# A group's feed-forward moved into the last beats of a delta rule, with the quantized layer two groups behind

## The chip, the core and the metric

The kernel runs as one program on one core of a Trainium2 chip. The metric is the device time of one execution in microseconds. Engine names are those of the profile: PE (TensorE matmul), PEld (its weight loads), DVE (VectorE), ACT (ScalarE), POOL (GpSimd), SP (SyncE, which here only issues DMAs).

## The reference

The input x is 16 sequences of 128 tokens with 256 features, all in float32. The computation is

```
a  = causal attention of x (16 heads of 16, a temperature per sequence)
x1 = x + delta_rule(a)          # gated delta rule: 16 key heads, 32 value heads of 128,
                                # causal convolution of 4 taps, chunks of 64, gated norm, W_out
f  = lora_ffn(x1, adapter of the sequence)
       gate = x1 Wg + (x1 Ag[i]) Bg[i];  up = x1 Wu + (x1 Au[i]) Bu[i]     # 256 -> 1024, rank 16
       h    = silu(gate) * up
       f    = h Wd + (h Ad[i]) Bd[i]                                       # 1024 -> 256
q  = quantized_ffn(f)           # weights rounded to float8 e4m3, 256 -> 768 -> 256
out = x1 + q
```

i is one of 8 adapters, drawn for each sequence.

## The kernel before

**Groups and units.** The 16 sequences are worked on in four groups (`NG`) of four (`GS`), 512 tokens each (`GT`). The delta rule has 64 units: 16 key heads for each group, in the order of groups. Everything is float32, so that TensorE takes two instructions for each product of a 128x128 block with 512 columns.

**The written order.** A beat of the delta rule (`BEAT`, 24 units of plan time) starts one unit. The steps of a unit have due times in `TIMES`, counted from its start: keys 0 to 32.5, decays, the inverse of a lower triangle for four units at once, mergers 178 to 187, `last` 194, values 177 to 195.5, outputs 217 to 236, finish 244 to 255.5. `plan` puts steps in a heap by due time and `run` issues them in that order, so in one beat steps of up to eleven units lie beside each other. The tile framework allocates the buffers, sets all semaphores, and fixes each engine's order when the program is compiled: by program order as a priority, and by when it reckons inputs and buffers to be ready. VectorE's order is tied to program order by hand (class `InOrder`, V). On ScalarE `silu_of` and `logarithms` tie the Silus and the blocks of Ln and Exp into an order, since they need different function tables.

**The end of a unit.** `attend` makes the outputs of a unit and their squares, `root` sums the squares, `share` (SP queue) writes the roots to DRAM (`scales`) and reads them back to all partitions as `rb`, 512 KB. `norm` (line 864, POOL) multiplies z by rb, and `project` (line 873, PE, 16 instructions) adds the unit's share of W_out to PSUM. After a group's last unit x is added and x1 is stored to DRAM (line 879).

**The buffers.** Pools are stacked. The delta rule's pools are c2 (cw, nw), w2 (w_qk), pc (Uc and Tc, cv, aT in 9 buffers, bT in 7, and small ones) and the `late` pools behind it (W, T, w_v, w_gate, wo_head, v, z, y, rb, x_in and others). ps_b has six PSUM buffers, ps_r two. `pa` and `keep` lie below them and stay. A pool opened after these are closed lies on the same addresses and waits for the last users of what it covers.

**The stage after.** `ffn_loads` is issued when the last inverse is done (plan time 1632). It loads wg and wu, the adapters of group 0 and x1 of group 0 into pa's buffers. After the delta rule's pools are closed, w3 (weights), p3 (work) and eight PSUM buffers (ps_x, ps_g) are opened. `adapted(g)` is the feed-forward with adapters in 14 steps: `turn` twice (transposes of x1, line 1074, and a copy to x1T), `low` (line 1081, and a mask on DVE), eight times `hidden` (lines 1091 and 1095; Silu on ACT, product on DVE), `low_down` (line 1106, and a mask), `down` twice (lines 1115 and 1116). `quantized(g)` has six `fuse` steps (lines 1134 and 1139) and two `down` (line 1148). `rounding` is nine steps that round the quantized weights with `qm` as scratch, on DVE and POOL; `behind` puts them after a product of `hidden`. `next_adapter(g)` gathers the adapters of a group by five indirect DMAs on POOL (lines 905 and 907) and rearranges them by a copy on ACT (line 910). `merge` interleaves lists evenly:

```python
for g in range(NG + 1):
    lists = []
    if g < NG:
        lists.append(adapted(g))
    if g == 0:
        lists.append([lambda: None] * 3 + [lambda f=f: behind(f) for f in rounding])
    else:
        lists.append(quantized(g - 1))
    if g + 1 < NG:
        lists.append(next_adapter(g + 1))
    merge(*lists)
```

So group 0 runs beside the rounding, groups 1 to 3 each beside the quantized part of the group before, and the quantized part of group 3 by itself.

Of the kernel before, what the change touches and what calls it, by code (L numbers as in the profile page):

```python
# [17 lines left out]
P = 128  # L18
# [40 lines left out]
def tile_adaln_attn_ffn(  # L59
# [108 lines left out]
    def attention():  # L168
# [47 lines left out]
        def project(g):  # L216
# [15 lines left out]

            def queries(e):
                if e == 0:
                    d["q"] = pc.tile([P, ND, GT], F32, name="qT", tag="Uc", bufs=2)
                A.copy(d["q"][:, e, :], product(wq_sb, e))

            def vals(i):
                if i == 0:
                    d["v"] = pc.tile([P, GS, D], F32, name="vt", tag="Tc", bufs=2)  # L240
# [366 lines left out]
    def inverse(n):  # L607
# [293 lines left out]

    def adapter(g, t, raw):

# [8 lines left out]
    def residual(g, t):  # L912
        nc.sync.dma_start(out=t, in_=x1[g * GS : (g + 1) * GS].rearrange("b s d -> s b d"))
        pre["x", g] = t

    pre = {}

# [49 lines left out]
    for n in range(N + LAST + 1):  # L967
# [37 lines left out]
        run(BEAT * (n + 1))  # L1005
        if n == N + 1 + int(TIMES["inverse"][-1] // BEAT):
            ffn_loads()
    run(BEAT * (N + LAST + 9))
    late["stack"].close()
    st.close()  # L1010


    with ExitStack() as st:
        w3 = st.enter_context(tc.tile_pool(name="w3", bufs=1))
        p3 = st.enter_context(tc.tile_pool(name="p3", bufs=2))
        ps_x = st.enter_context(tc.tile_pool(name="ps_x", bufs=4, space=PSUM))
# [16 lines left out]


        def quantize(t, n):
            m = w3.tile([P, QI * ND], F32, name="qm", tag="qm")[:, :n]

            def step():
                V.tensor_scalar(m.bitcast(I32), t.bitcast(I32), 0x7F800000, None, ALU.bitwise_and)
# [6 lines left out]
            def checked():  # L1046
# [11 lines left out]
        grp3 = {}  # L1058

        def masked(dst, ps):  # L1060

            V.tensor_tensor(dst.rearrange("p (s t) -> p s t", t=S), ps.rearrange("p (s t) -> p s t", t=S),
                            fourth[:, :, None].to_broadcast([P, GS, S]), ALU.mult)

        def adapted(g):
            d = grp3[g] = {}

            def turn(c):
                if c == 0:
                    d["x"] = p3.tile([P, ND, GT], F32, name="x1T", tag="x1T")  # L1070
                    d["h"] = p3.tile([P, NFI, GT], F32, name="hid", tag="hid", bufs=1)
                ps = ps_x.tile([P, GS, S], F32, name="ps_xt", tag="x")
                for s in range(GS):
                    T.transpose(ps[:, s, :], pre["x", g][:, s, c * P : (c + 1) * P], ident)  # L1074
                A.copy(d["x"][:, c, :], ps.rearrange("p s t -> p (s t)"))

            def low():
                ps = ps_x.tile([P, GT], F32, name="ps_low", tag="x")
                for c in range(ND):
                    w = pre["a", g][:, 2 * c : 2 * c + 2].rearrange("p j s r -> p (j s r)")  # L1080
                    T.matmul(ps, lhsT=w, rhs=d["x"][:, c, :], start=c == 0, stop=c == ND - 1)  # L1081
                d["low"] = p3.tile([P, GT], F32, name="low", tag="low")
                masked(d["low"], ps)

            def hidden(i):
                cols = slice(i * P, (i + 1) * P)
                both = []
                for w in ("wg", "wu"):
                    ps = ps_g.tile([P, GT], F32, name="ps_gu", tag="g")
                    for c in range(ND):  # L1090
                        T.matmul(ps, lhsT=pre[f"{w}{c}"][:, cols], rhs=d["x"][:, c, :], start=c == 0, stop=False)  # L1091
                    both.append(ps)

                for ps, half in zip(both, HALVES):
                    T.matmul(ps, lhsT=pre["b", g][half, cols], rhs=d["low"][half, :], start=False, stop=True)  # L1095
                gs = p3.tile([P, GT], F32, name="gs", tag="gs")
                A.activation(gs, both[0], AF.Silu)
                grp3["product"] = V.tensor_tensor(d["h"][:, i, :], both[1], gs, ALU.mult)

            def low_down():  # L1100


                ps = ps_x.tile([P, GT], F32, name="ps_ld", tag="x")
                for i in range(NFI):
                    w = pre["a", g][:, 2 * ND + i].rearrange("p s r -> p (s r)")
                    T.matmul(ps[HALVES[i % 2]], lhsT=w, rhs=d["h"][:, i, :], start=i < 2, stop=i >= NFI - 2)  # L1106
                d["ld"] = p3.tile([P, GT], F32, name="ld", tag="ld")
                masked(d["ld"], ps)
                d["y"] = p3.tile([P, ND, GT], F32, name="yT", tag="yT")

            def down(e):
                ps = ps_x.tile([P, GT], F32, name="ps_y3", tag="x")
                cols = slice(e * P, (e + 1) * P)
                for i in range(NFI):
                    T.matmul(ps, lhsT=wd_sb[:, i, cols], rhs=d["h"][:, i, :], start=i == 0, stop=False)  # L1115
                T.matmul(ps, lhsT=pre["b", g][:, FI + e * P : FI + (e + 1) * P], rhs=d["ld"], start=False, stop=True)  # L1116
                A.copy(d["y"][:, e, :], ps)

            return (
                [lambda: turn(0), lambda: turn(1), low]  # L1120
                + [lambda i=i: hidden(i) for i in range(NFI)]
                + [low_down, lambda: down(0), lambda: down(1)]
            )

        def quantized(g):
            d = grp3[g]
# [32 lines left out]
            with tc.issue_after(grp3["product"].ins):  # L1159
                f()  # L1160

        def next_adapter(g):
            d = grp3["next"] = {}

            def gather():
                d["arrange"] = adapter(g, p3.tile([P, GS * LA + LB], F32, name="adapters", tag="adapters"),
                                       w3.tile([P, GS * LA], F32, name="firsts", tag="firsts"))

            return [gather, lambda: d["arrange"]()]
# [76 lines left out]
```

## Time and profile before

| what | value |
|---|---|
| time, median of 3 runs | 2249.76 us (2246.99 to 2257.99) |
| the profiled execution: time, span | 2258.01 us, 2256.3 us |
| mean granted clock of TensorE | 0.98 |
| PE busy | 2127.2 us, 94% of the span, 15992 instructions |
| PEld busy | 1297.5 us, 58% |
| DVE busy | 1404.9 us, 62% |
| ACT busy | 1365.7 us, 61% |
| POOL busy | 831.6 us, 37% |
| DMA | 182.14 MB, 81 GB/s in the mean |

The profile is of one execution; its times start at the first instruction. PE's busy time is modelled from the instructions' starts, so overlapping matmuls count as one stretch. A line such as L873 is a line of the kernel; L79 is the helper that issues every operation of VectorE, so there the tile's name tells what it is. `x16` is a number of instructions. In brackets stand the idle time of the engine before an instruction and what ended it.

### The profile page before, as it was taken

To read this page: it belongs to the slowest core of one execution; us is meant where nothing else is said; L and a number is where in the kernel's file an instruction comes from. 1 tells how busy PE (TensorE), PEld (TensorE's weight loads), DVE (VectorE), ACT (ScalarE), POOL (GpSimd) and SP (SyncE) were. 2 spreads that over 40 slices of the span, in tenths; PEclk is the share of its full clock that TensorE was granted. 3 is DMA by queue.
4 is the path that set the end of the run, shared out by engine and by line. 5 is a ranking of instruction groups with operands and counts; after the bars stand their busy time and mean duration, and the time that the engine had idled before them with its cause. 6 is when DMAs were issued, how large, how long until landed. Compare 5 with 4: busy or idle time off the path is not lost. (4 is left out here: it accounts for less than half of the span.)

```text
span 2256.3 us, 41245 instructions
## 1 busy us (share of the span) xinstructions
PE 2127.2 (94%) x15992; PEld 1297.5 (58%) x15992; DVE 1404.9 (62%) x2194; ACT 1365.7 (61%) x2373; POOL 831.6 (37%) x573
## 2 busy tenths in 40 slices
PE   7898689999999999999999999999998987999999
PEld 3444356666666666666666666666665663344445
DVE  4788887677686867768686777868665321311111
ACT  4778577777777777777777777777775661111110
POOL 2233535445262544526254452625444115400000
PEclk9999889999999999999999999999999998999999
DMA  2210123333334434333433433334333314000000
GB/s 60 70 44 25 55 64 88 96 103 100 96 107 113 112 93 107 98 97 107 114 111 93 107 99 96 106 101 115 93 103 94 99 56 153 0 5 17 10 5 14
DMA packets 303250, 182.14 MB, mean 81 GB/s; under 512 B 189393, under 2 KB 283345, under 8 KB 303057
## 3 DMA queue, kind: packets, MB, share of 16 engines
q1 hardware_dynamic: 300848, 175.00, 28.0%
q0 software_dynamic: 1344, 4.20, 0.6%
q8 instruction: 128, 2.10, 0.4%
q14 instruction: 66, 0.53, 0.1%
q10 hardware_dynamic: 864, 0.31, 0.1%
HBM read 152.69 MB, written 5.77 MB: 70 GB/s over the span
## 5 line engine op out<-in xcount | busy, mean ns | idle before, releaser
L79 DVE SCALAR_TENSOR_TENSOR cv<-ps_in,cw,cv 128x508 f32<-128x508 f32 (+2 forms) x768 | 567.1, 740 | 297.4 <-ACT cv L476 279.3
L873 PE MATMUL ps_out<-wo_head,z 128*128 128x256 f32 x1024 | 251.7, 390 | 35.7 <-POOL z L864 35.5
L864 POOL TENSOR_TENSOR z<-z,rb 128x1024 f32<-128x1024 f32 x64 | 151.2, 2362 | 310.9 <-DMA rb<-scales 264.7
L467 PE MATMUL ps_in<-hT,w_qk 128*128 128x512 f32 x512 | 249.0, 610 | 5.3 <-DVE cv L79 2.4
L467 PE MATMUL ps_in<-hT,w_v 128*128 128x512 f32 x512 | 248.6, 607 | 0.0
L873 PEld LDWEIGHTS ps_out<-wo_head,z 128*128 128x128 f32 x1024 | 190.7, 194 | 99.6 <-POOL z L864 67.8
L812 PE MATMUL ps_z<-hT,w_gate 128*128 128x512 f32 x512 | 241.9, 594 | 0.3 <-ACT M L776 0.3
L476 ACT ACTIVATE cv<-ps_in,cw 128x512 f32<-128x512 f32 x256 | 174.9, 683 | 77.9 <-PE ps_in L467 76.3
L638 POOL TENSOR_TENSOR prod<-lanes,inv 128x512 f32<-128x512 f32 (+1 forms) x64 | 129.5, 2045 | 121.3 <-DVE inv L79 121.3
L525 POOL TENSOR_TENSOR o<-off,lk 128x16 f32<-128x16 f32 x64 | 13.9, 217 | 414.8 <-ACT lk L555 414.8
L812 PEld LDWEIGHTS ps_z<-hT,w_gate 128*128 128x128 f32 x512 | 95.8, 190 | 114.4 <-issue 101.1
L829 PEld LDWEIGHTS ps_ot<-aT,y 128*128 128x128 f32 x1024 | 134.5, 192 | 38.1 <-issue 28.5
L586 PE MATMUL ps_kq<-kq 128*128 128x256 f32 x512 | 134.8, 407 | 15.4 <-DVE cv L79 14.0
L467 PEld LDWEIGHTS ps_in<-hT,w_qk 128*128 128x128 f32 x512 | 94.1, 195 | 85.9 <-issue 66.5
L823 PEld LDWEIGHTS ps_y<-v,W 128*128 128x128 f32 x1024 | 124.5, 192 | 30.6 <-issue 22.9
L570 ACT ACTIVATE kq<-cv 128x512 f32<-128x512 f32 x128 | 80.7, 630 | 97.8 <-DVE cv L79 97.6
L829 PE MATMUL ps_ot<-aT,y 128*128 128x128 f32 x1024 | 135.6, 275 | 1.7 <-ACT y L824 1.7
L638 POOL TENSOR_TENSOR prod<-inv,gm 128x512 f32<-128x512 f32 (+1 forms) x64 | 127.9, 2023 | 15.3 <-DVE gm L79 15.3
L823 PE MATMUL ps_y<-v,W 128*128 128x128 f32 x1024 | 124.8, 275 | 0.0
L467 PEld LDWEIGHTS ps_in<-hT,w_v 128*128 128x128 f32 x512 | 87.5, 190 | 64.1 <-issue 61.2
L529 POOL TENSOR_TENSOR aT<-aT,o 128x1024 f32<-128x1024 f32 x64 | 121.8, 1902 | 5.1
L586 PEld LDWEIGHTS ps_kq<-kq 128*128 128x128 f32 x512 | 94.7, 197 | 34.5 <-issue 9.4
(202 smaller groups left out, 4069.0 us busy)
## 6 DMA issues: line engine op xcount, KB each, us to landing
aT<-sums SPq DMA_DIRECT2D x64, 512.0 KB
rb<-scales SPq DMA_DIRECT2D x64, 512.0 KB
w_qk<-in_w_qkv_dram SPq DMA_DIRECT2D x128, 128.0 KB
w_v<-in_w_qkv_dram SPq DMA_DIRECT2D x64, 256.0 KB
w_gate<-in_w_z_dram SPq DMA_DIRECT2D x64, 256.0 KB
wo_head<-in_w_out_dram SPq DMA_DIRECT2D x64, 256.0 KB
diag<-bT SPq DMA_DIRECT2D x256, 32.0 KB
W<-Uc SPq DMA_DIRECT2D x256, 32.0 KB
```

The source lines that it names most:

```text
L79: ins = getattr(self.engine, name)(*args, **kw)
L467: T.matmul(ps, lhsT=w[:, c, blk, :], rhs=hTs[g][:, c, :], start=c == 0, stop=c == ND - 1)
L476: A.activation(cv, psv, AF.Copy, scale=cw[:, col, 3:4])
L529: G.tensor_tensor(t4, t4, o.rearrange("p s h i -> p (s h) i")[:, :, :, None].to_broadcast([P, NP, 2, C]), ALU.subtract)
L570: ins = A.activation(dst, src, AF.Silu)
L586: T.matmul(ps[:, j, :, :], lhsT=d["kq"][:, s, 0, :], rhs=d["kq"][:, s, :, :], start=True, stop=True)
L638: G.tensor_tensor(out_tile, lhs[:, :, None, :].to_broadcast([P, r, c, j]), rhs.rearrange("p j c -> p c j")[:, None, :, :].to_broadcast([P, ...
L812: T.matmul(ps, lhsT=w_gate[u][:, c, h * P : (h + 1) * P], rhs=hTs[g][:, c, :], start=c == 0, stop=c == ND - 1)
L823: T.matmul(ps[:, j, :], lhsT=d["W"][:, p, :], rhs=v[:, p, :], start=True, stop=True)
L829: T.matmul(ps[:, s * S : (s + 1) * S], lhsT=d["y"][:, 2 * s + h, :], rhs=d["aT"][:, 2 * s + h, :], start=True, stop=True)
L864: G.tensor_tensor(d["z"], d["z"], d["rb"], ALU.mult)
L873: T.matmul(ps[:, j, :], lhsT=d["z"][:, h, s * S : (s + 1) * S], rhs=w_o[u][:, h, :], start=kh == j == h == 0, stop=kh == NK - 1 and j == h ...
```

## The change

1. Group 0's feed-forward with adapters (`adapted(0)`) is no longer in the stage after. Its 14 steps are planned into the delta rule's last beats at due times of their own (`DRAIN_TIMES`, 1639.2 to 1758.6). It works in the delta rule's buffers (class `Drain`): PSUM from ps_b; x1T, the two low ranks, the gates and the down weights in bT's buffers, the hidden rows in aT's, and its result yT in one of hT's.
2. The down weights wd are loaded for it in two halves of 512 KB (plan times 1689.6 and 1692), and once more as wd_sb after the delta rule as before.
3. x1 of group 1 is loaded in `ffn_loads`, into the buffer of `off`.
4. Uc and Tc get a pool of their own, pi, ahead of pc. After the delta rule the order of pools is w0 (adapters, 2 buffers, and their raw form), p2 (x1T, hid, low, gs, ld of groups 1 to 3), w3, p3. `next_adapter(1)` is issued first there.
5. `qm` has three buffers instead of one.
6. The stage after runs over g = 1 to 5: group 1 beside the rounding, group 2 beside the quantized part of group 0, group 3 beside that of group 1, then the quantized parts of groups 2 and 3 one after the other.

`adapted`, `masked` and `next_adapter` are otherwise as they were: buffers come from an object `room`, which is a `Drain` or a `Rest`.

```diff
@@ pools
     w2 = st.enter_context(tc.tile_pool(name="w2", bufs=2))
+    pi = st.enter_context(tc.tile_pool(name="pi", bufs=2))
     pc = st.enter_context(tc.tile_pool(name="pc", bufs=1))
...
-                    bt["T"] = pc.tile([P, BL, BL], F32, name="Tc", tag="Tc", bufs=2)
+                    bt["T"] = pi.tile([P, BL, BL], F32, name="Tc", tag="Tc")
...
-            bt["U"] = pc.tile([P, BL, BL], F32, name="Uc", tag="Uc", bufs=2)
+            bt["U"] = pi.tile([P, BL, BL], F32, name="Uc", tag="Uc")
...
@@ ffn_loads
         residual(0, pa.tile([P, GS, D], F32, name="x1_in", tag="diag"))
+        residual(1, keep.tile([P, GS, D], F32, name="x1_in", tag="off", bufs=1))
...
+    def adapted(g, room):
+        d = grp3[g] = {}
+        def turn(c):
+            if c == 0:
+                d["x"] = room.x()
+                d["h"] = room.hidden()
+            ps = room.ps("ps_xt", "x").rearrange("p (s t) -> p s t", t=S)
...
+        def hidden(i):
...
+                ps = room.ps("ps_gu", "g")
...
+            gs = room.gs(i)
+            A.activation(gs, both[0], AF.Silu)
+            grp3["product"] = V.tensor_tensor(d["h"][i], both[1], gs, ALU.mult)
...
+        def down(e):
+            ps = room.ps("ps_y3", "x")
+            cols = slice(e * P, (e + 1) * P)
+            for i in range(NFI):
+                T.matmul(ps, lhsT=room.down(i)[:, cols], rhs=d["h"][i], start=i == 0, stop=False)
...
+    class Drain:
+        def __init__(self):
+            self.both = {}
+        def ps(self, name, tag):
+            return ps_b.tile([P, GT], F32, name=name, tag="b")
+        def x(self):
+            return pc.tile([P, ND, GT], F32, name="x1T", tag="bT", bufs=7)
+        def hidden(self):
+            parts = [pc.tile([P, 2, GT], F32, name="hid", tag="aT", bufs=9) for _ in range(NFI // 2)]
+            return [parts[i // 2][:, i % 2, :] for i in range(NFI)]
+        def half(self, name, i):
+            if name not in self.both:
+                self.both[name] = pc.tile([P, 2, GT], F32, name=name, tag="bT", bufs=7)
+            return self.both[name][:, i, :]
+        def low(self, name):
+            return self.half("lows", 0 if name == "low" else 1)
+        def gs(self, i):
+            return self.half("gs", i % 2)
+        def y(self):
+            return keep.tile([P, ND, GT], F32, name="yT", tag="hT", bufs=2)
+        def load_down(self, i):
+            t = self.both["wd", i] = pc.tile([P, 4, D], F32, name="wd_sb", tag="bT", bufs=7)
+            nc.sync.dma_start(out=t, in_=wd.rearrange("(c p) e -> p c e", p=P)[:, 4 * i : 4 * i + 4])
+        def down(self, i):
+            return self.both["wd", i // 4][:, i % 4, :]
...
+    DRAIN_TIMES = [1639.2, 1644.0, 1648.2, 1653.0, 1662.6, 1672.2, 1681.8, 1699.8, 1699.8, 1717.8, 1729.8, 1739.4, 1749.0, 1758.6]
...
         if n == N + 1 + int(TIMES["inverse"][-1] // BEAT):
             ffn_loads()
+            drain = Drain()
+            plan(0, adapted(0, drain), DRAIN_TIMES)
+            plan(0, [lambda i=i: drain.load_down(i) for i in range(2)], [24 * 70.4, 24 * 70.5])
...
@@ the stage after
+        w0 = st.enter_context(tc.tile_pool(name="w0", bufs=1))
+        p2 = st.enter_context(tc.tile_pool(name="p2", bufs=2))
         w3 = st.enter_context(tc.tile_pool(name="w3", bufs=1))
         p3 = st.enter_context(tc.tile_pool(name="p3", bufs=2))
...
+        for f in next_adapter(1):
+            f()
-        for g in range(1, NG):
+        for g in range(2, NG):
             residual(g, w3.tile([P, GS, D], F32, name=f"x1_in{g}", tag=f"x1_in{g}"))
...
-            m = w3.tile([P, QI * ND], F32, name="qm", tag="qm")[:, :n]
+            m = w3.tile([P, QI * ND], F32, name="qm", tag="qm", bufs=3)[:, :n]
...
+        class Rest:
+            def ps(self, name, tag):
+                return (ps_g if tag == "g" else ps_x).tile([P, GT], F32, name=name, tag=tag)
+            def x(self):
+                return p2.tile([P, ND, GT], F32, name="x1T", tag="x1T")
...
+            def y(self):
+                return p3.tile([P, ND, GT], F32, name="yT", tag="yT")
...
-        for g in range(NG + 1):
+        for g in range(1, NG + 2):
             lists = []
             if g < NG:
-                lists.append(adapted(g))
-            if g == 0:
+                lists.append(adapted(g, Rest()))
+            if g == 1:
                 lists.append([lambda: None] * 3 + [lambda f=f: behind(f) for f in rounding])
             else:
-                lists.append(quantized(g - 1))
+                lists.append(quantized(g - 2))
             if g + 1 < NG:
                 lists.append(next_adapter(g + 1))
             merge(*lists)
```

More of the change, by code (lines that the diff above doesn't have):

```diff
@@ L234, in queries @@
                 if e == 0:
-                    d["q"] = pc.tile([P, ND, GT], F32, name="qT", tag="Uc", bufs=2)
+                    d["q"] = pi.tile([P, ND, GT], F32, name="qT", tag="Uc")
                 A.copy(d["q"][:, e, :], product(wq_sb, e))
@@ L239, in vals @@
                 if i == 0:
[L240 removed]
+                    d["v"] = pi.tile([P, GS, D], F32, name="vt", tag="Tc")
                 ps = ps_b.tile([P, 2, D], F32, name="ps_v", tag="b")
@@ L914, in residual, with masked, low, low_down @@
         pre["x", g] = t
+    grp3 = {}
+    def masked(dst, ps):
+        V.tensor_tensor(dst.rearrange("p (s t) -> p s t", t=S), ps.rearrange("p (s t) -> p s t", t=S),
+                        fourth[:, :, None].to_broadcast([P, GS, S]), ALU.mult)
+    def adapted(g, room):
[5 more added lines that the diff above has]
+            ps = room.ps("ps_xt", "x").rearrange("p (s t) -> p s t", t=S)
+            for s in range(GS):
+                T.transpose(ps[:, s, :], pre["x", g][:, s, c * P : (c + 1) * P], ident)
+            A.copy(d["x"][:, c, :], ps.rearrange("p s t -> p (s t)"))
+        def low():
+            ps = room.ps("ps_low", "x")
+            for c in range(ND):
+                w = pre["a", g][:, 2 * c : 2 * c + 2].rearrange("p j s r -> p (j s r)")
+                T.matmul(ps, lhsT=w, rhs=d["x"][:, c, :], start=c == 0, stop=c == ND - 1)
+            d["low"] = room.low("low")
+            masked(d["low"], ps)
+        def hidden(i):
+            cols = slice(i * P, (i + 1) * P)
+            both = []
+            for w in ("wg", "wu"):
+                ps = room.ps("ps_gu", "g")
+                for c in range(ND):
+                    T.matmul(ps, lhsT=pre[f"{w}{c}"][:, cols], rhs=d["x"][:, c, :], start=c == 0, stop=False)
+                both.append(ps)
+            for ps, half in zip(both, HALVES):
+                T.matmul(ps, lhsT=pre["b", g][half, cols], rhs=d["low"][half, :], start=False, stop=True)
+            gs = room.gs(i)
+            A.activation(gs, both[0], AF.Silu)
+            grp3["product"] = V.tensor_tensor(d["h"][i], both[1], gs, ALU.mult)
+        def low_down():
+            ps = room.ps("ps_ld", "x")
+            for i in range(NFI):
+                w = pre["a", g][:, 2 * ND + i].rearrange("p s r -> p (s r)")
+                T.matmul(ps[HALVES[i % 2]], lhsT=w, rhs=d["h"][i], start=i < 2, stop=i >= NFI - 2)
+            d["ld"] = room.low("ld")
+            masked(d["ld"], ps)
+            d["y"] = room.y()
+        def down(e):
+            ps = room.ps("ps_y3", "x")
+            cols = slice(e * P, (e + 1) * P)
+            for i in range(NFI):
+                T.matmul(ps, lhsT=room.down(i)[:, cols], rhs=d["h"][i], start=i == 0, stop=False)
+            T.matmul(ps, lhsT=pre["b", g][:, FI + e * P : FI + (e + 1) * P], rhs=d["ld"], start=False, stop=True)
+            A.copy(d["y"][:, e, :], ps)
+        return (
+            [lambda: turn(0), lambda: turn(1), low]
+            + [lambda i=i: hidden(i) for i in range(NFI)]
+            + [low_down, lambda: down(0), lambda: down(1)]
+        )
@@ L1022, in loaded, with next_adapter, gather @@
             return t
-        for g in range(1, NG):
+        def next_adapter(g):
+            d = grp3["next"] = {}
+            def gather():
+                d["arrange"] = adapter(g, w0.tile([P, GS * LA + LB], F32, name="adapters", tag="adapters", bufs=2),
+                                       w0.tile([P, GS * LA], F32, name="firsts", tag="firsts"))
+            return [gather, lambda: d["arrange"]()]
+        for f in next_adapter(1):
+            f()
+        for g in range(2, NG):
             residual(g, w3.tile([P, GS, D], F32, name=f"x1_in{g}", tag=f"x1_in{g}"))
@@ L1056, in tile_adaln_attn_ffn @@
                     + quantize(dq.rearrange("p c e -> p (c e)"), NQI * D))
[L1058 to L1123, printed above, removed]
@@ L1160, in behind, with hidden, low, gs @@
                 f()
[L1162 to L1169, printed above, removed]
-        for g in range(NG + 1):
+        class Rest:
[3 more added lines that the diff above has]
+                return p2.tile([P, ND, GT], F32, name="x1T", tag="x1T")
+            def hidden(self):
+                t = p2.tile([P, NFI, GT], F32, name="hid", tag="hid", bufs=1)
+                return [t[:, i, :] for i in range(NFI)]
+            def low(self, name):
+                return p2.tile([P, GT], F32, name=name, tag=name)
+            def gs(self, i):
+                return p2.tile([P, GT], F32, name="gs", tag="gs")
+            def y(self):
+                return p3.tile([P, ND, GT], F32, name="yT", tag="yT")
+            def down(self, i):
+                return wd_sb[:, i, :]
+        for g in range(1, NG + 2):
             lists = []
             if g < NG:
-                lists.append(adapted(g))
-            if g == 0:
+                lists.append(adapted(g, Rest()))
+            if g == 1:
                 lists.append([lambda: None] * 3 + [lambda f=f: behind(f) for f in rounding])
             else:
-                lists.append(quantized(g - 1))
+                lists.append(quantized(g - 2))
             if g + 1 < NG:
```

## The prediction

> **What bounds the kernel now.** I read the page's slices first, then busy time by stretch, then the timeline around the stage change, then the chain that ended last. The row of TensorE's busy share, 40 slices of 56.4 us:
>
> ```profile
> PE   7898689999999999999999999999998987999999
> ```
>
> Only the start and slices 30 to 33 (1692 to 1918 us) fall short of nine tenths: the end of the delta rule, and the change of stage. So I cut the run into the steady delta rule, its last beats, the wait for the last unit, the gap to the first hidden matmul, group 0 alone, and the rest (columns: stretch, length, busy PE, PEld, DVE, ACT, POOL, clock, DMA share, GB/s):
>
> ```profile
> 451.20:1635.60 1184.40, 1158.23 (x10371) 766.82 (x10370) 884.26 (x1398) 868.26 (x1537) 524.69 (x360) 1.00 0.38 103
> 1784.00:1863.70 79.70, 73.17 (x651) 50.84 (x652) 20.47 (x32) 46.49 (x83) 11.72 (x7) 0.98 0.22 66
> 1863.70:1881.70 18.00, 7.40 (x25) 5.63 (x23) 0.69 (x2) 0.00 (x0) 3.85 (x3) 0.62 0.82 279
> 1881.70:1889.00 7.30, 3.57 (x4) 1.51 (x5) 0.69 (x1) 1.80 (x3) 2.81 (x3) 0.67 0.66 159
> 1889.00:1948.50 59.50, 58.00 (x151) 22.29 (x150) 22.57 (x22) 7.48 (x11) 38.91 (x18) 0.98 0.09 32
> 1948.50:2250.70 302.20, 302.17 (x864) 142.09 (x862) 43.61 (x61) 38.86 (x62) 17.68 (x11) 1.00 0.03 9
> ```
>
> TensorE is the bound nearly everywhere: 97.8% busy in the steady part, 100% from 1948.5 on. Moving matmuls can only win where it idles or is slowed: 6.5 us in 1784 to 1863.7, most of 1863.7 to 1889, 1.5 in the group alone. The timeline says why (start, length, instruction, [idle before, releaser]):
>
> ```profile
> 1860.11 3.72 PE L873 MATMUL ps_out<-wo_head,z 128*128 128x256 f32 x16 [0.58 <-POOL z L864]
> ...
> 1872.88 2.34 POOL L864 TENSOR_TENSOR z<-z,rb 128x1024 f32<-128x1024 f32 x1 [7.36 <-DMA rb<-scales]
> ...
> 1875.27 6.39 PE L873 MATMUL ps_out<-wo_head,z 128*128 128x256 f32 x16 [10.56 <-POOL z L864]
> ...
> 1884.79 1.07 ACT L1075 COPY x1T<-ps_xt 128x512 f32<-128x512 f32 x2 [23.83 <-DMA x<-x_in]
> ...
> 1885.43 3.78 PE L1081 MATMUL ps_low<-x1T,adapters 128*128 128x512 f32 x4 [3.77 <-ACT x1T L1075]
> ```
>
> The last unit's projection waits 10.56 us for its normalizers' round trip through DRAM and then runs at half speed (6.39 for what took 3.72 before it). Group 0's first copy then waits for the last store of the delta rule, because its buffer lies in a pool that overlaps it. On VectorE one more wait stands in the group alone:
>
> ```profile
> 1937.00 0.96 DVE L79 TENSOR_SCALAR qm<-dq 128x1536 int32<-128x1536 int32 x1 [8.19 <-POOL uq L1050]
> ```
>
> It is the single buffer qm. The masked low rank stands behind it in VectorE's order, and TensorE waited 1.5 us for that. Prices of the moved work come from the chain, which is pure PE there:
>
> ```profile
> 1940.74 6.87 PE ps_y L1115 x16
> 1947.60 0.86 PE ps_y L1116 x2
> ...
> 1958.01 3.43 PE ps_gu L1091 x8
> 1961.44 1.06 PE ps_gu L1095 x4
> ...
> 2014.44 3.58 PE ps_ld L1106 x16
> ```
>
> **One group (A) and one quantized part (Q).** A: turn 1.04 (1863.67), low 1.80 (1952.77), eight hidden steps of 3.43 + 1.06 = 35.9, low_down 3.58, two downs of 6.87 + 0.86 = 15.5: 57.8 us. Q: six fuse steps of 3.44 and two downs of 5.38: 31.4. Three A and four Q make 299.0, against 302.2 measured from 1948.5 to 2250.7, so the prices hold to 1%.
>
> **The change, part by part.** The profiled execution took 2258.0 us (span 2256.3 and 1.7 around it), 8.2 above the median; the sum is made against it and the difference carried to 2249.8.
>
> *Group 0 into the drain.* The planner's slots 1639.2 to 1758.6 stand against unit 58's norm (planned 1636, real 1781.5) and unit 63's (1756, 1872.9): real time 1784 to 1875. Weights are there (the last wu issue is at 1755.3, the copied adapters at 1757.3). All of A but the two downs, 42.3 us, goes ahead of 1863.7. Without any filling that stretch would be 79.7 + 42.3 = 122.0; with the steady share of 97.8% it is (73.2 + 42.3) / 0.978 = 118.1, so 3.9 is filled. The two downs, 15.5 us, come between unit 62's and unit 63's projection. The round trip is over 11.6 us after the former (1863.67 to 1875.27), and shorter without the weight loads: rb landed in 3.9 us for unit 62 (1853.84 to 1857.70) and in 7.7 for unit 63 with four loads beside it. So that wait vanishes, and with it the half clock: 2.7 (6.39 - 3.72). End of the drain: 57.8 - 3.9 - 11.6 - 2.7 = 39.6 later, at 1921.3.
>
> What else rides along. ACT gets two turn copies, eight Silus at 0.60 and two copies, 7.1 us, on 46.5 of 79.7; DVE ten operations of 0.69, 6.9 us, on 20.5: nothing, hidden by TensorE. If that cover went, the dearest wait of TensorE on ACT inside a unit in this stretch is 0.8 us (ps_ot for y); 14 pieces at that price are 11 us, and no wait at all would win 2.6 more (6.5 - 3.9). I take the steady share, since those beats have the same six PSUM buffers and more work of the other engines. The SP queue gets residual(1) and two halves of wd, with scales, rb and W placements queued behind; their buffers were last read in earlier beats (unit 61's `last` at 1658, the load at 1689.6), so they wait for nothing: 0, or 3.8 once if an rb lands beside them as unit 63's did.
>
> ScalarE also switches function tables in the drain, nine loads of 1.28 us in 1784 to 1863.7, the next instruction following at once (load at 1839.27, copy at 1840.56). The new Silus are not tied into that order. Two more loads for each of the eight would be 20.5 us of ACT: 74.1 of 118, still no bound. "ScalarE: Activation LUTs", What ACT_TABLE_LOAD costs, of the Trainium skill speaks against the change here: it puts a switch at 2.66 us, half of it a drain, and asks to group by table. By that price the same sixteen would be an estimated 42.6 us, and ACT 96 of 118, near a bound.
>
> *New start of the rest.* The gap of 7.3 us (1881.7 to 1889.0) becomes group 1's turn, copy and low. The new pool p2 lies on attention and decay buffers, not on x_in, so the copy waits only for the drain's last down, and the clock is full: 1.04 + 1.1 + 1.80 = 3.9, a gain of 3.4. If the turn slips ahead of the last projection it is 1.8. If the gathers of group 1's adapters were held until the drain ended, 6.4 (issue at 1886.86 to copy at 1893.21) + 0.8 + 1.8 = 9.0; w0 (19.5 KB a partition) fits on cw, w_qk and the new pool pi (21.5 KB), free 15 us earlier, so I take 3.9. POOL's queue has these gathers ahead of unit 63's z: five at 1.25 from 1860.8 end at 1867, before rb lands.
>
> The quantized weights' loads now wait for the drain's tiles, thus begin at about the last projection instead of 18 us before its end. They are hidden: gq is first touched 7.6 us after the first hidden matmul (1896.6), wd_sb 36 after. If gq's 768 KB came 4 us late, DVE would stand with the products behind it: 4.
>
> *Group 1 alone with the rounding.* As group 0 was, 59.5, less the 1.5 (three qm buffers) and less 1.0 for the first matmuls at half clock: 57.0, a gain of 2.5.
>
> *The rest.* Three A and four Q become two A and four Q: 57.8 less. Two Qs alone instead of one cost nothing: the lone Q ran 31.2 us without a wait. The buffers taken over from hT (yT) and off (x1 of group 1) had their last readers in the key steps, before 1784: no wait, nothing.
>
> **Sum:** +39.6 - 3.4 - 2.5 - 57.8 = -24.1. 2258.0 becomes 2233.9, the median 2249.8 becomes 2225.7. Own bounds: 2.6 + 2.1 + 2.2 (the wait of 2.18 at 1783.93, if the first turn fills it) more gain, about -31, or 2219; 11 us of filler waits less, -13, or 2237.
>
> **Rivals.** *Slower: PSUM slots held by ACT.* Each hidden step holds two of six ps_b buffers until Silu and product are done. If each Silu meets two table loads, the pair comes back after 2 x 1.28 + 0.60 + 0.69 = 3.85 us, and if the next matmuls always need that slot, eight stalls are 30.8: +6.7 net, 2256.5. It decides from 3.0 us a step (24.1 / 8). For it: no order ties these Silus to the table blocks. Against: ACT idles 33 of 79.7 us there, and ps_in and ps_kq of the key stage no longer take slots.
>
> *Same: the gain is eaten in small pieces.* 11 of filler waits, 3.8 for an rb beside wd, 5.1 for late adapters (9.0 - 3.9): -24.1 + 19.9 = -4, 2245.6. For it: the last units are chains of short steps, and TensorE takes its queue in order. Against: the steady beats are such chains too, at 97.8%.
>
> *Same: it doesn't do what it says.* The engines' order is fixed at compile time by readiness; if the pieces end up behind the last unit, only 3.4 + 2.5 remain: 2243.9. Against: their inputs are ready before 1784.
>
> **How the numbers follow.** Forecast 0.71; the two "same" rivals 0.12 and 0.05; the slower one 0.12. A measurement of this kernel can tell 0.5% (11 us) from no change; the forecast's bounds, 13 to 31, lie beyond that. Predicted: 2226. The forecast's own range, 2219 to 2237, is widened for the three runs' spread (2247 to 2258) below to 2213 and into the "same" cases above to 2246.
>
> **What would show it.** Right: the 10.56 us wait before unit 63's ps_out gone and its 16 matmuls near 3.7; x1T's copy of group 1 no longer waiting for the store; no DVE wait of 8 us at qm; from the last projection to the last quantized matmul 3.9 + 57.0 + 244 us. Wrong: PE waits on gs, hid or y of several us in the drain, more than nine table loads there with PE idle behind them, PE idle after the last projection for adapters or gq.

## The result and the profile after

The changed kernel took 2221.84 us in the median (2219.49 to 2224.2, 4 runs), the kernel before 2252.93 beside it (2246.99 to 2257.99, 4 runs): a ratio of 0.9862, 95% interval 0.9846 to 0.9877. The prediction was 2226.0 with a range of 2213 to 2246; the time lies inside, and the likeliest case is the one that came. Three later groups of runs of the changed kernel have medians of 2226.78, 2230.35 and 2227.61, all inside too. The profiled execution took 2219.49 us (span 2217.8, mean granted clock 0.987).

TensorE's slices in the page of the changed kernel, 40 of 55.4 us:

```profile
PE   7898689999999999999999999999999899999999
```

Around the end of the delta rule one slice reads below 9 (the 32nd). Before there were three, the 31st, 33rd and 34th; the 32nd, which the prediction counts with them, reads 9 in its row. The stretches, cut at the same events as before: unit 58's norm to the end of unit 62's projection, that to the end of unit 63's, the gap to the first hidden matmul of group 1, group 1 alone, the rest (columns: stretch, length, busy PE, PEld, DVE, ACT, POOL, clock, DMA share, GB/s):

```profile
1771.10:1890.20 119.10, 114.62 (x796) 67.28 (x800) 28.93 (x44) 61.85 (x99) 11.77 (x6) 0.99 0.16 48
1890.20:1909.90 19.70, 19.70 (x63) 10.21 (x63) 1.11 (x2) 3.67 (x6) 14.66 (x14) 1.00 0.51 166
1909.90:1912.90 3.00, 2.71 (x13) 1.51 (x12) 0.69 (x1) 2.36 (x3) 0.94 (x1) 1.00 1.02 355
1912.90:1969.40 56.50, 56.50 (x149) 21.72 (x148) 31.89 (x22) 5.36 (x9) 32.22 (x10) 1.00 0.22 68
1969.40:2212.30 242.90, 242.88 (x705) 119.20 (x703) 36.67 (x51) 31.84 (x50) 17.96 (x11) 1.00 0.03 11
```

From unit 62's projection on, TensorE idles 0.3 us up to the last matmul; the clock is at or above 0.99 in every row (the 18.0 us that the second row replaces had 7.40 busy at a clock of 0.62). The timeline around the last unit:

```profile
1890.70 7.13 PE L976 MATMUL ps_y<-hid,wd_sb 128*128 128x512 f32 x16
...
1903.21 2.35 POOL L865 TENSOR_TENSOR z<-z,rb 128x1024 f32<-128x1024 f32 x1 [0.77 <-DMA rb<-scales]
...
1906.26 3.62 PE L874 MATMUL ps_out<-wo_head,z 128*128 128x256 f32 x16
...
1910.40 1.07 ACT L936 COPY x1T<-ps_xt 128x512 f32<-128x512 f32 x2 [3.36 <-PE ps_xt L935]
...
1911.04 1.98 PE L942 MATMUL ps_low<-x1T,adapters 128*128 128x512 f32 x4 [0.29 <-ACT x1T L936]
```

No bracket stands behind `ps_out`: it follows the second down without a wait, and its 16 matmuls run at full clock (1.00 in the row above; they take 3.62, before there were 10.56 of wait and 6.39). The copy to x1T waits for the transposes, no longer for the store of x1. All waits of PE between 1760 and 1920 (line, releaser, us in total, times, longest):

```profile
PE ps_out L874 <- POOL z L865: 4.8, 3, 2.8
PE ps_low L942 <- ACT x1T L936: 0.3, 1, 0.3
```

**A measure that leaves the start out.** On every engine the instructions come in the same order in both kernels up to the first inserted one, on TensorE 1765 us in and on SP 1686. Yet unit 57's norm starts at 1761.34 in the profiled execution of before and at 1751.15 in that of after; three other executions of the same changed kernel have 1758.65, 1760.83 and 1761.21. Those 10 us are a difference between executions, and 7.6 of them are there before anything was inserted: the last transfer ahead of it on SP is issued at 1692.66 before and at 1685.03 after. So each trace below is also read from the start of unit 57's norm to the end of its span. That stretch is 495.0 us before, and 466.65, 466.45, 466.8 and 466.7 in four executions of the changed kernel: the change takes 28.3 us off. Of the kernel before there is one trace, so its 495.0 has no spread of its own.

### The profile page after: what moved, and what is told of

Same layout as the page of the kernel before. It is cut to its first block, busy times and chain, and to the rows that moved or that the text cites. A ratio compares the mean times of both kernels' runs of the same rounds, so it can differ in the third digit from the quotient of the medians.

```text
span 2217.8 us, 41241 instructions
## 1 busy us (share of the span) xinstructions
PE 2111.8 (95%) x15992; PEld 1292.4 (58%) x15992; DVE 1413.3 (64%) x2194; ACT 1374.3 (62%) x2379; POOL 831.7 (38%) x573
## 4 chain that ended last, share of the span: by engine, by line
PE 51%; DVE 15%; issue 11%; DMA 8%; POOL 8%; ACT 4%; SPq 2%; POOLq 0%; DVEq 0%; ACTq 0%
PE ps_in L468 11%; PE ps_out L874 8%; DMA rb<-scales 5%; PE ps_z L813 5%; PE ps_ot L830 4%; DVE cv L79 4%; POOL prod L639 4%; PE ps_gu L952 4%; PE ps_kq L587 3%; POOL z L865 3%; PE ps_y L824 2%; PE ps_vt L796 2%; PE ps_lv L771 1%; PE ps_lo L738 1%; DVE inv L79 1%
## 5 line engine op out<-in xcount | busy, mean ns | idle before, releaser
L571 ACT ACTIVATE kq<-cv 128x512 f32<-128x512 f32 x128 | 80.7, 630 | 97.8 <-DVE cv L79 97.7
L834 ACT ACTIVATE sq<-ps_ot 128x512 f32<-128x512 f32 x128 | 75.7, 591 | 68.7 <-PE ps_ot L830 67.8
```

## Experiments

Times are medians. "Stretch" is the measure just described: start of unit 57's norm and end of the span give it for each run.

| run | time us | ratio to before | stretch us |
|---|---|---|---|
| before | 2253.76, 2256.28 and 2258.11 beside the three groups of runs | 1 | 2256.3 - 1761.34 = 495.0 |
| e1_no_drain | 2248.02 | 0.9978 (0.9964 to 0.9991) | 2244.8 - 1755.91 = 488.9 |
| e2_downs_forced | 2244.72 | 0.9962 (0.9947 to 0.9977) | 2239.2 - 1756.01 = 483.2 |
| e3_p2_last | 2235.24 | 0.9917 (0.9902 to 0.9933) | 2233.8 - 1759.71 = 474.1 |
| e4_after_again | 2226.78 | 0.9882 (0.9865 to 0.9899) | 2225.1 - 1758.65 = 466.45 |
| e5_after_ref | 2230.35 | 0.9886 (0.9867 to 0.9906) | 2227.6 - 1760.83 = 466.8 |
| e6_earlier | 2219.89 | 0.985 (0.9828 to 0.9871) | 2214.4 - 1753.69 = 460.7 |
| e7_silus_tied | 2224.42 | 0.9854 (0.9834 to 0.9874) | 2225.5 - 1760.86 = 464.6 |
| e8_qm_one | 2229.39 | 0.9884 (0.9864 to 0.9903) | 2228.4 - 1759.63 = 468.8 |
| e9_after_third | 2227.61 | 0.9862 (0.9838 to 0.9887) | 2227.9 - 1761.21 = 466.7 |
| e10_both | 2219.28 | 0.9831 (0.9811 to 0.9851) | 2218.0 - 1758.20 = 459.8 |
| e11_two_and_one | 2227.21 | 0.9864 (0.984 to 0.9887) | 2227.8 - 1761.35 = 466.45 |

e1 to e4 ran together, e5 to e8, and e9 to e11. e4, e5 and e9 are the changed kernel again, as the measure of their group.

### Group 0 left after the delta rule, all else as changed

```diff
-            drain = Drain()
-            plan(0, adapted(0, drain), DRAIN_TIMES)
-            plan(0, [lambda i=i: drain.load_down(i) for i in range(2)], [24 * 70.4, 24 * 70.5])
...
-        for g in range(1, NG + 2):
+        for g in range(NG + 1):
...
-            if g == 1:
+            if g == 0:
                 lists.append([lambda: None] * 3 + [lambda f=f: behind(f) for f in rounding])
             else:
-                lists.append(quantized(g - 2))
+                lists.append(quantized(g - 1))
-            if g + 1 < NG:
+            if 1 < g + 1 < NG and g > 0:
                 lists.append(next_adapter(g + 1))
```

> Group 0 goes back to the stage after, beside the rounding, with the quantized part one group behind as before; the new pools (pi, w0, p2), three qm buffers, and x1 of group 1 in off's place stay. Theory 1 (the change wins where moved matmuls fill TensorE's idle time at the end of the delta rule): only the two small terms remain, -3.4 (x1T no longer waits for the last store) and -2.5 (qm, first matmuls at full clock), so -6 us against the kernel before, about 2247 by its median of 2252.9, ratio 0.997; ps_out of unit 63 waits again some 10 us for z and runs at half clock. Theory 2 (the new start of the stage after, pools and qm, is most of the gain): -15 us or more, ratio 0.993 or less.

Measured: 6.1 us less than before in the stretch (495.0 - 488.9), 5.7 in the medians (2253.76 - 2248.02). Pools, qm and early loads alone give the 6 of theory 1; the other 22 of the 28.3 us come with group 0's move. The 6.1 is not made up as expected, though. From the end of unit 62's projection to the first hidden matmul 20.0 us stand for 25.3 before, and group 0 alone takes 56.8 for 59.5, together 8.0 less; but the same work from unit 58's norm to unit 62's projection took 83.9 for 82.2, at a clock of 0.96 for 0.98, which takes 1.7 back. The waits of PE at 1860 to 1890 in this run show what the move takes away:

```profile
PE ps_low L942 <- ACT x1T L936: 5.4, 1, 5.4
PE ps_out L874 <- POOL z L865: 3.1, 1, 3.1
PE ps_gu L952 <- DVE x_in L79: 0.8, 1, 0.8
```

Without the store in its way group 0's first low rank slips into the round trip of the last unit, but it is too little work to fill it. That is why unit 63's projection waits 3.1 us here and not the 10 that were expected, and why the gap shrinks by 5.3 and not by 3.4.

### The two downs behind the last projection

```diff
-DRAIN_TIMES = [..., 1739.4, 1749.0, 1758.6]
+DRAIN_TIMES = [..., 1739.4, 1767.6, 1767.7]
...
-            plan(0, adapted(0, drain), DRAIN_TIMES)
...
+            fs = adapted(0, drain)
+            plan(0, fs[:-2] + [lambda f=f: after_last(f) for f in fs[-2:]], DRAIN_TIMES)
```

`after_last` issues a step after the last matmul of unit 63's projection.

> As the changed kernel, but the two downs of group 0 are tied behind unit 63's last projection on TensorE, with due times 1767.6 and 1767.7; the other twelve steps stay in their slots. Theory 1: TensorE has nothing between unit 62's and unit 63's projection, waits 11.6 to 14.7 us for z (in the changed kernel z was done 15.3 us after unit 62's projection, with ten gathers ahead of it on POOL), and runs 16 matmuls at half clock, 2.7 us: +14 to +17 us against the changed kernel, 2236 to 2239, ratio 0.993. Theory 2: no more than +3, 2225.

Measured: 16.6 us more than the changed kernel in the stretch, 17.9 in the medians. The timeline of this run:

```profile
1907.29 2.35 POOL L865 TENSOR_TENSOR z<-z,rb 128x1024 f32<-128x1024 f32 x1
...
1909.70 5.22 PE L874 MATMUL ps_out<-wo_head,z 128*128 128x256 f32 x16 [14.14 <-POOL z L865]
...
1914.75 7.03 PE L976 MATMUL ps_y<-hid,wd_sb 128*128 128x512 f32 x16
```

The same 15.5 us of matmuls, one place later: a wait of 14.14 is back, and with it a projection of 5.22 for 3.62. Group 1's first transposes wait 0.68 more, for the copy of yT; the three make 16.4 of the 16.6. So more than half of the change's gain hangs on where two of its 14 pieces stand.

### The pool of x1T back on the delta rule's x_in

```diff
-        p2 = st.enter_context(tc.tile_pool(name="p2", bufs=2))
         w3 = st.enter_context(tc.tile_pool(name="w3", bufs=1))
         p3 = st.enter_context(tc.tile_pool(name="p3", bufs=2))
+        p2 = st.enter_context(tc.tile_pool(name="p2", bufs=2))
```

> As the changed kernel, with pool p2 opened after p3, so that x1T, hid, low, gs and ld of groups 1 to 3 lie on the late pools, x_in among them; every engine's order is the same. My prediction's term: group 1's x1T copy waits for the last store of x1 again; in the changed kernel that store is issued at 1910.6 and x1T is written at 1910.4 to 1911.5, so the copy would go at about 1913.5 to 1914.6: +3 us, and up to +5 if TensorE falls to half clock: 2225 to 2227. Rival: the wait of 23.8 us in the kernel before was for POOL or DVE and not for the store, then 0.

Measured: 7.6 us more in the stretch, 8.5 in the medians, more than either theory had. Every engine's order is that of the changed kernel; only addresses differ. The timeline of this run:

```profile
1915.16 0.51 SPq L1136 DMA_DIRECT2D gq<-in_gate_w_dram  x1
...
1917.19 2.08 SPq L880 DMA_DIRECT2D x<-x_in  x2
...
1923.57 1.07 ACT L936 COPY x1T<-ps_xt 128x512 f32<-128x512 f32 x2 [8.24 <-DMA x<-x_in]
...
1924.20 3.78 PE L942 MATMUL ps_low<-x1T,adapters 128*128 128x512 f32 x4 [5.17 <-ACT x1T L936]
```

The copy is again released by the store. The store is issued in two halves, at 1917.19 and 1918.91, and 4.7 us passed from the second to the copy (6.4 from the first), where it was 2.4 in the kernel before. Loads issued some 2 us ahead of it, gq (768 KB) and x1 of another group (512 KB), were under way beside it (DMA share 1.01, 360 GB/s from 1918.0 to 1927.8). That they lengthened the store fits both traces; it was not tried apart. Behind the wait came half clock (0.50 in 1924.2 to 1927.9): 3.78 instead of 1.98, and 3.03 instead of 1.88 for the first four ps_gu. A wait 4.9 longer (5.17 - 0.29) and 1.8 and 1.15 of half clock make 7.85, beside 7.6 measured.

### One buffer for qm

```diff
-            m = w3.tile([P, QI * ND], F32, name="qm", tag="qm", bufs=3)[:, :n]
+            m = w3.tile([P, QI * ND], F32, name="qm", tag="qm")[:, :n]
```

> The rounding's scratch qm has one buffer again instead of three; every engine's order is that of the changed kernel. Theory 1 (the third buffer took VectorE's 8 us wait at qm away, and with it a wait of TensorE): an 8 us wait of VectorE is back in group 1's part and TensorE waits 1.5 us for the masked low rank ahead of its ps_y; 56.5 us of group 1 alone become 58; of the whole, 1.5 us more. Rival (with the order of groups changed something else hides it): the wait of VectorE is back and TensorE's part stays at 56.5.

Measured: 2.1 us more in the stretch; the medians (2229.39 against 2230.35) cannot tell it. The timeline of this run, DVE and then PE:

```profile
1968.77 0.96 DVE L79 TENSOR_SCALAR qm<-dq 128x1536 int32<-128x1536 int32 x1 [8.26 <-POOL uq L1176]
...
1970.64 0.68 DVE L79 TENSOR_TENSOR ld<-ps_ld,fourth 128x512 f32<-128x512 f32 x1
...
1971.38 1.12 PE L977 MATMUL ps_y<-ld,adapters 128*128 128x512 f32 x2 [1.57 <-DVE ld L79]
```

This is the wait of before in its old size (8.19 and 1.50). VectorE waits for a buffer, the masked low rank queues behind it, and TensorE meets that. Group 1 alone took 58.1 us for 56.5, so 1.6 of the 2.1 stand where theory 1 had them; the other 0.5 is near the spread of the measure. Theory 1.

### The drain's Silus tied into ScalarE's order

```diff
-            A.activation(gs, both[0], AF.Silu)
+            (silu_of if isinstance(room, Drain) else lambda o, i: A.activation(o, i, AF.Silu))(gs, both[0])
```

> The eight Silus of group 0 in the drain are tied into the order of ScalarE's other Silus, so that none falls between a Ln and an Exp: six table loads fewer (167 to 161), 7.7 us of ScalarE at 1.28 each. No other engine's order differs. Theory 1 (ScalarE is off the path in the drain): 0, within 2 us. Theory 2, the prediction's slower rival (ScalarE's table loads hold the PSUM buffers that TensorE needs): up to 7.7 us less, ratio to the changed kernel down to 0.9965.

Measured: 2.0 us less in the stretch (5.9 in the medians, most of which lies ahead of unit 57 or in the spread of 4 and 5 runs). The groups of ScalarE's table loads, in the changed kernel first:

```profile
L958 ACT ACT_TABLE_LOAD x3 | 3.8, 1283 | 0.1
L553 ACT ACT_TABLE_LOAD x2 | 2.6, 1283 | 0.0
L554 ACT ACT_TABLE_LOAD x2 | 2.6, 1283 | 0.0
```

and in this run:

```profile
L958 ACT ACT_TABLE_LOAD x1 | 1.3, 1283 | 0.0
```

Six loads are gone, 7.7 us of ScalarE, and 2.0 of them reach the end. Where most of it comes from can be seen at unit 62. In the changed kernel a load stands between the Ln and the Exp that make its normalizers:

```profile
1868.80 0.42 ACT L553 ACTIVATE r<-r 128x256 f32<-128x256 f32 x1 [0.89 <-DVE r L79]
1869.23 1.28 ACT L554 ACT_TABLE_LOAD   x1
1870.53 0.42 ACT L554 ACTIVATE r<-r 128x256 f32<-128x256 f32 x1
...
1880.92 1.99 PE L874 MATMUL ps_out<-wo_head,z 128*128 128x256 f32 x8 [1.47 <-POOL z L865]
```

and in this run none does:

```profile
1877.72 0.42 ACT L553 ACTIVATE r<-r 128x256 f32<-128x256 f32 x1 [1.38 <-DVE r L79]
1878.17 0.42 ACT L554 ACTIVATE r<-r 128x256 f32<-128x256 f32 x1
...
1888.66 1.99 PE L874 MATMUL ps_out<-wo_head,z 128*128 128x256 f32 x8 [0.29 <-POOL z L865]
```

The wait for unit 62's norm is 1.2 shorter, about one load; the other 0.8 was not located. So table loads did reach TensorE, where theory 1 had 0 within 2 us, but by another path than theory 2's: they delayed a norm. The wait for PSUM buffers that theory 2 had is in neither trace: from 1745 to 1925 TensorE waits for no gate, hidden row or buffer of the drain. ScalarE's slack swallowed three quarters of the six loads. "ScalarE: Activation LUTs", What ACT_TABLE_LOAD costs, of the Trainium skill puts a switch at 2.66 us, half of it a drain, which would make these six an estimated 16 us of ScalarE. Measured, its busy time between unit 57's norm and the first down fell by 7.66 (75.30 to 67.64), 1.28 each. In the rows above the engine was idle for 0.1 us in all before the seven loads, so no drain shows beside them, and the rows decide.

### The first four pieces and low_down earlier

```diff
-DRAIN_TIMES = [1639.2, 1644.0, 1648.2, 1653.0, 1662.6, ..., 1739.4, 1749.0, 1758.6]
+DRAIN_TIMES = [1633.0, 1635.0, 1638.0, 1641.0, 1662.6, ..., 1737.2, 1749.0, 1758.6]
```

> The first four pieces of group 0 (both turns, low, the first hidden step) are due 6 to 12 units of plan time sooner, so that they stand ahead of unit 58's projection, and low_down ahead of unit 62's; nothing else moves. In the changed kernel TensorE still waits 2.8 us for unit 58's z and runs its 16 matmuls about 1.6 us over the full clock's time, and waits 1.5 us for unit 62's z. Theory 1 (whatever is ready fills a wait, and takes the slow clock behind it away too): 4 to 6 us less than the changed kernel, ratio to it 0.9975. Rival (the pieces are late themselves there, or push the steps that the next units wait for, so that the wait only changes place): 0, within 2 us.

Measured: 5.9 us less in the stretch, 10.5 in the medians (2230.35 - 2219.89; the stretch is the safer figure). Unit 57's norm to the first down of the drain, in the changed kernel:

```profile
1751.15:1890.70 139.55, 133.58 (x968) 79.93 (x966) 35.32 (x54) 75.30 (x123) 14.63 (x7) 0.99 0.19 54
```

and in this run:

```profile
1753.69:1887.33 133.64, 131.11 (x967) 78.72 (x965) 35.23 (x53) 74.82 (x123) 14.61 (x7) 1.00 0.20 57
```

The same work in 5.9 us less: idle time falls from 6.0 to 2.5, and busy time by 2.5, as the clock rises from 0.99 to 1.00. In the changed kernel unit 58's projection waited 2.77 us and its first eight matmuls took 3.62; here hidden step 0 stands ahead of them and they take 1.89, which is 1.7 of the 2.5. Theory 1.

### Both together

The edits of the two runs above, in one kernel.

> The earlier due times of the first four pieces and of low_down, and the drain's Silus tied into ScalarE's order, together. From the norm of unit 57 to the end the earlier due times alone took 460.7 us and the tied Silus alone 464.6, against 466.6 of the changed kernel. Theory 1 (both win by filling the same few waits of TensorE ahead of the projections, of which the earlier due times leave 2.5 us): 459 to 461, no sum of the two. Rival (they win apart): 458.7 or less. Of the whole 0.996 to 0.997 of the changed kernel.

Measured: 459.8 us in the stretch, 0.9 less than the earlier pieces alone, and 2219.28 beside 2227.61 of the changed kernel (2258.11 of before). The two edits fill the same waits, as theory 1 has it. This is the fastest version, 0.9831 of before (0.9811 to 0.9851), though only the 0.9 us of the stretch tells it from e6_earlier (0.985, 0.9828 to 0.9871).

### The quantized part caught up, one left for the end

```diff
-        for g in range(1, NG + 2):
+        for g in range(1, NG + 1):
...
-                lists.append(quantized(g - 2))
+                lists.append([f for k in {2: (0,), 3: (1, 2), 4: (3,)}[g] for f in quantized(k)])
```

> The quantized part catches up: group 3's feed-forward runs beside the quantized parts of groups 1 and 2 instead of group 1 alone, and only group 3's quantized part is left for the end instead of two. Theory 1 (TensorE is busy all the time in either order, so how far behind the quantized part runs costs nothing): 0, within 1 us from the norm of unit 57 to the end. Rival (two quantized parts alone are dearer, for example by their waits on Silu and VectorE, or three streams together hold each other's PSUM buffers): 1 to 5 us, to either side.

Measured: 466.45 us in the stretch against 466.7, and 2227.21 beside 2227.61. Theory 1: whether one quantized part or two are left for the end costs nothing, and gains nothing.

### The changed kernel again

> The changed kernel unaltered, as the measure for the others of this call: 2222 by its own four runs (ratio 0.986), its profile with unit 57's z between 1751 and 1761 if the 10 us by which the two profiles differ before the change's first instruction on TensorE are differences between executions. If they belong to the change, unit 57's z is at 1751 again.

> The changed kernel once more, as the measure for the three runs beside it. Both theories: the ratio of its first comparisons again, 0.986 to 0.988, some 2225 us.

> The changed kernel once more, as the measure for the two runs beside it. Both theories: ratio 0.986 to 0.989, and 466.6 us from the norm of unit 57 to the end of the span, as in its three profiled executions so far (466.65, 466.45, 466.8).

The ratios of the three are 0.9882, 0.9886 and 0.9862: 26 to 31 us less than before, around the 28.3 of the stretch. The first two lie a little above what was expected (0.986, and 0.986 to 0.988). Unit 57's norm in e4_after_again, at 1758.65, puts the 10 us down to executions.

## Why the prediction was right, point by point

From unit 58's norm to the end the traces show 474.8 us before and 446.7 after, 28.1 less; the sum was 24.1. The mechanism was the one forecast, and the 4 us are four terms:

| term | predicted | measured |
|---|---|---|
| drain, unit 58's norm to the end of unit 63's projection | +39.6 | 100.2 to 138.8: +38.6 |
| new start | -3.4 | 7.3 to 3.0: -4.3 |
| group alone | -2.5 | 59.5 to 56.5: -3.0 |
| rest | -57.8 | 302.2 to 242.9: -59.3 |

- **Drain.** Up to unit 62's projection 36.9 was added (82.2 to 119.1) for 42.3 of work, where 38.4 was forecast. The prediction's own cut began at unit 58's projection; by it the stretch is 116.7 for the 118.1 forecast. The two turns (1.04) stand ahead of unit 58's norm, at 1765 and 1770, and delay nothing (that norm starts 20.0 us after unit 57's, 20.2 before). The rest is idle time: TensorE was busy for 114.62 of those 116.68, 98.2% for the steady share of 97.8%. e6_earlier shows that 5.9 more were to be had by due times alone. From unit 62's projection on the forecast was +1.2 (15.5 - 11.6 - 2.7) and the trace shows +1.7.
- **The cover of the last round trip was thinner than written.** 11.6 us were to lie under 15.5 of downs. Unit 63's norm ended 15.4 us after unit 62's projection (1905.56 after 1890.2): its rb landed at 1903.2, 13.0 us after instead of 9.2. The traces say why. Before, the sum of unit 63's squares stood ahead of unit 62's projection on TensorE (which ran from 1860.11 to 1863.67):

```profile
1858.89 0.64 PE L842 MATMUL ps_r<-sq,ones 128*32 128x256 f32 x8 [0.69 <-ACT sq L833]
...
1860.99 2.58 SPq L850 DMA_DIRECT2D scales<-r  x4
...
1865.18 0.33 SPq L852 DMA_DIRECT2D rb<-scales  x1
```

After, it stands behind that projection, which ended at 1890.2:

```profile
1890.13 0.64 PE L843 MATMUL ps_r<-sq,ones 128*32 128x256 f32 x8
...
1892.24 2.56 SPq L851 DMA_DIRECT2D scales<-r  x4
...
1896.49 0.34 SPq L853 DMA_DIRECT2D rb<-scales  x1
```

So rb was issued 6.3 us after unit 62's projection instead of 1.5. That step of the prediction was wrong: it took the round trip over as it was. From its issue rb took 6.7 us, less than the 7.7 of before but far from the 3.9 that the prediction hoped for without the weight loads; the DMA share in that time was 0.90. Ten adapter gathers, of groups 1 and 2, were under way beside it, twice the five that the prediction counted; that they slowed rb was not tried apart. On POOL they ended at 1902.45, before rb was there, and did not hold the norm in this execution. In e5_after_ref the norm began directly behind the last of them. The norm ended 0.7 us before unit 63's projection began, in e4_after_again 0.2: that the longer trip still fitted under the downs was luck.
- **New start.** The copy waits for the transposes only, as forecast; the 3.9 became 3.0 because only one turn and one copy stand in the chain (0.45 of transposes, 0.59 of copy, 1.98 of low); the other half runs beside them. e3_p2_last shows that the address of one pool is worth 7.6 here, more than the 3.4 that the prediction gave to it: with the drain in front, loads are issued just ahead of the store and run beside it.
- **Group alone.** TensorE's idle time went from 1.5 to 0, as forecast for qm (e8_qm_one: 1.6 in this part). Its busy time fell from 58.0 to 56.5 as the clock rose from 0.98 to 1.00, so the half clock at the first matmuls was worth 1.5 and not 1.0.
- **Rest.** The price of A was low. The chain of the changed kernel, group 1 alone:

```profile
1913.03 3.43 PE ps_gu L952 x8
1916.46 1.06 PE ps_gu L956 x4
1917.52 3.63 PE ps_gu L952 x8
```

A hidden step that follows another hidden step takes 0.2 more than one behind another piece, and A was priced by the cheaper kind. Three of eight steps of an interleaved group are of the dear kind, 0.6 of the 1.5. The other 0.9 stands in the same chain of before: a gate step of the quantized part takes 0.19 more when it follows a hidden step, which four of the six beside a group do, and the first of the two downs, behind low_down, takes 7.06 for the 6.87 of the second.

```profile
1954.57 1.72 PE ps_qg L1134 x4
...
1962.50 1.91 PE ps_qg L1134 x4
```

- **The rivals.** PSUM slots held by ACT: of the waits that it needs none shows. Fifteen table loads stand between unit 58's norm and unit 62's projection where nine stood before, which the prediction named among the signs of being wrong; the six cost 2.0 us and not 30.8, mostly through a norm (e7_silus_tied). Small pieces: TensorE waited for no adapters, and its idle time there fell from 8.7 to 4.5. That it doesn't do what it says: without the drain 6.1 remain, close to the 5.9 that this rival had been given.

## What to carry to other kernels

Work that is ready is worth most where the bounding engine waits longest: put a piece at least as long as a round trip between its start and its reader, and measure what is left, since 15.5 us of matmuls ahead of the last projection instead of behind it were worth 16.6. Add to a wait what a slow clock behind it costs: 4.9 of wait brought 2.95 of slower matmuls in e3_p2_last. When a pool is opened on addresses that a store still reads, the first write waits for that store, and loads issued beside it may make that longer. When work is put in front of a last step, look also at what it pushes back: here the sum of squares that starts the last round trip came later, and the cover was nearly used up.

## What the runs showed of the hardware

- The granted clock fell after some short waits and not after others. At unit 58's projection, after 2.77 to 3.16 us without a matmul, the first eight matmuls, 1.89 to 1.99 us elsewhere, took 2.45 to 3.62 (3.62 in the changed kernel, at a clock of 0.53 in 1773.5 to 1777.1). At an earlier projection of the same kernel they took 1.99 after a wait of 2.96 (e9_after_third, at 1710.61) and 3.78 after one of 2.91 (e5_after_ref, at 1709.23). After 5.17 us four matmuls of 1.98 took 3.78 (e3_p2_last); after 14.14 us sixteen of 3.62 took 5.22 (e2_downs_forced, clock 0.71).
- Matmuls with 64 rows of weights (`ps_gu`, 64*128) are followed in the changed kernel by a weight load with 0.76 us of idle before it (at 1917.45), where 0.24 is usual, and the next step takes longer: 3.63 instead of 3.43, or 1.91 instead of 1.72.
- Executions of the changed kernel differ by up to 10 us in the first 1760 us, with the same instructions in the same order, and by 0.35 us in the 466 that follow (four executions). Other kernels can differ more there: from unit 58's norm to unit 62's projection the same work took 83.9 us in e1_no_drain and 82.2 before. A small edit late in a kernel is better read from a common event than from the whole time.
